# Multiplications by B half a unit ahead of their scans in place of a whole unit

## The chip, the cores and the metric

The kernel runs on one core of one Trainium2 chip. The metric is the time of one execution on the device, in microseconds (us), given as the median of several runs. The engines of the core are named as in the profile: PE (TensorE, with PEld for its weight loads), DVE (VectorE), ACT (ScalarE), POOL (GpSimd) and SP (SyncE, which here issues transfers).

## The reference

The reference is a network of four layers on four images of 64 x 64 positions with 96 channels. The last two layers are attention and a quantised feed-forward network; the change does not touch them. The first two are selective scans in four directions, and that is where the change lies. For each direction k, each of E = 192 channels and each of 16 states, the layer computes a recurrence over the 4,096 positions:

```python
def step(h, inp):
    u, d, b, c = inp
    dA = jnp.exp(d[..., None] * A)
    h = dA * h + d[..., None] * b[:, :, None, :] * u[..., None]
    y = jnp.einsum('bken,bkn->bke', h, c)
    return (h, y)
```

Here `d` is a step size computed from the image, `u` the image itself, `b` and `c` vectors of 16 states for each position. The input of the recurrence is thus the product of `d * u` (one value for each channel and position) and `b` (one value for each state and position).

## The kernel before

The kernel handles the two scan layers in four phases: two layers, each for two pairs of images. Each phase has a preparation (`prepare`: statistics, convolution, step sizes), in which `d * u` is written to memory as `du` and the step sizes as `delta`, and then a scan phase (`scan_phase`). Between them the outputs of the phase before are finished. After the fourth phase come the token layers.

A scan phase runs over 128 units: 8 chunks (`NC`) of 512 positions (`TC`), and in each chunk 16 blocks (`NEB`) of `EB` = 12 channels. The 128 partitions hold two images, four directions and 16 states. A unit passes through these steps:

- `load` fetches `dlt` (L375) and `h` (L390) through SP's queue: `h` is filled with `du`, in six transfers of 512 KB. There are four buffers of `h`. The loads of unit i+2 are recorded at the end of unit i-1 (step 11).
- `times_b` (L401, POOL) multiplies `h` by the chunk's B, in four instructions for each unit, each on `ER` = 3 of its 12 rows.
- `replicate` (L407, PE) spreads a row of `dlt` over the partitions, and `decay` (L411, ACT) makes the factor `a` of it. They run three to four rows ahead of the scan (`LEAD`).
- `scan` (L418, DVE) computes the recurrence of one row in place, from `a` in PSUM and `h` in SBUF, with the state `carry` of the chunk before. There are 12 scans in each unit.
- `contract` (L436, PE) multiplies the finished rows of the unit before by C, `evict` (L448, ACT) copies the results out, and `store` (L456) writes them with four transfers through SP's queue.
- `load_b` and `load_c` fetch B and C of a later chunk (L343); `weights` (L359, ACT) lays out C for the contractions.

The whole phase stands under `manual_schedule`: each engine executes its own instructions in the order in which the Python code records them. An instruction waits, by semaphores, for what writes its inputs and for what last uses the memory that it overwrites. The order of recording is the loop over units (`at`) and steps (`n` from 0 to 11, with `t = at * EB + n`), and `b_at(t)` is called once for each step, after the step's scan.

Of the kernel before, what the change touches and what calls it, by code (L numbers as in the profile page):

```python
# [32 lines left out]
EB = 12  # L33
NEB = E // EB
ER = EB // 4
# [5 lines left out]
NF = HID // 128  # L41
EPS = 1e-5
LEAD = 4
LN_EXP = "natural_log_exp_and_others"
SQRT_HALF = 0.7071067811865476

# [80 lines left out]
class Scans:  # L127
# [333 lines left out]
    def scan_phase(self, ph):  # L461

        nc = self.nc
        units = [self.Unit(ph, c, eb) for c in range(NC) for eb in range(NEB)]
        last = len(units)

        def ahead(t, do):
            at, n = divmod(t, EB)  # L470
            if at < last:
                do(units[at], n)

        def b_at(t):
            at, n = divmod(t, EB)
            if n % ER == 0 and 0 <= at + 1 < last:
                self.times_b(units[at + 1], n // ER)

        with self.tc.tile_pool(name="units", bufs=2) as self.units, self.tc.tile_pool(
            name="p_a", bufs=6, space=PSUM  # L480
        ) as self.p_a, self.tc.tile_pool(name="p_y", bufs=2, space=PSUM) as self.p_y:
            with self.tc.manual_schedule():
                self.start_phase(ph)
                self.load_b(ph, 0)
                self.load(units[0])
                self.load_c(ph, 0)
                self.load(units[1])
                self.load(units[2])
                self.load_c(ph, 1)
                for t in range(-EB, 0, ER):  # L490
                    b_at(t)
                for op in range(16):
                    self.weights(ph, 0, op)
                for t in range(LEAD):
                    ahead(t, self.replicate)
                for t in range(LEAD - 1):
                    ahead(t, self.decay)
                for at, u in enumerate(units):
                    before = units[at - 1] if at else None
                    for n in range(EB):  # L500
                        t = at * EB + n
                        ahead(t + LEAD, self.replicate)
                        ahead(t + LEAD - 1, self.decay)
                        self.scan(u, n)
                        q, part = divmod(n, 3)
                        if before:
                            if part < 2:
                                self.contract(before, q, part)
                            else:
                                self.evict(before, q)  # L510
                            if n == 4 and before.c < NC - 1:
                                e = before.eb * EB
                                nc.scalar.copy(
                                    ph.carry[:, e : e + EB], before.h[:, :, TC - 1]
                                )
                        b_at(t)
                        if n == 1 and u.eb >= 2 and u.c + 1 < NC:
                            self.weights(ph, u.c + 1, u.eb - 2)
                        if n == 7 and u.eb >= NEB - 2 and u.c + 1 < NC:
                            self.weights(ph, u.c + 1, u.eb)  # L520
                        if n == EB - 1:
                            if before:
                                self.store(before)
                            if u.eb == 8 and u.c + 1 < NC:
                                self.load_b(ph, u.c + 1)
                            if u.eb == NEB - 1 and u.c + 2 < NC:
                                self.load_c(ph, u.c + 2)
                            if at + 3 < last:
                                self.load(units[at + 3])
                for q in range(4):  # L530
                    self.contract(units[-1], q, 0)
                    self.contract(units[-1], q, 1)
                    self.evict(units[-1], q)
                self.store(units[-1])
# [178 lines left out]
def token_layers(ctx: ExitStack, tc, cst, a, layers, x_in, x_out):  # L713
# [51 lines left out]
    def layernorm(t, cut, out, first, **quant):  # L765
# [6 lines left out]
        with ExitStack() as order:  # L772
# [4 lines left out]
            if first:  # L777
                nc.scalar.preload_act_table_set(LN_EXP)
        var = p_a.tile([128, TC], F32, name="pa")
# [199 lines left out]
```

## Time and profile before

| what | value |
|---|---|
| median of 3 runs | 12,560.81 us |
| lowest and highest of them | 12,543.26 and 12,572.67 us |
| profiled execution, its own time | 12,532.27 us |
| profiled execution, its span | 12,530.5 us |
| PE busy | 9,786.3 us (78%) |
| DVE busy | 9,408.2 us (75%) |
| POOL busy | 7,413.5 us (59%) |
| ACT busy | 7,029.5 us (56%) |
| moved by DMA | 2,491.55 MB, mean 199 GB/s |

The span runs from the first instruction to the last of one profiled execution; its own time is 1.8 us more. The shares are means over the whole span, in which the scan phases alternate with the preparations, and the token layers follow from about 11,340 us on. What a change in the scan phases is worth must therefore be read from views cut to those phases. In a row of the groups stand the line, the engine, the operation, what it writes and reads, the number of instructions, then their busy time and the mean duration of one in ns, then the idle time of the engine just before them and what ended it.

### The profile page before, as it was taken

The numbers are of one execution on the slowest core, as the hardware profiler recorded it, in microseconds if no ns is written. First come the engines' busy times: TensorE is split into PE (matmuls) and PEld (weight loads), VectorE is DVE, ScalarE is ACT, GpSimd is POOL, SyncE is SP. The second block draws the span as 40 slices with busy tenths as digits, with TensorE's granted clock in tenths as the row PEclk, the third lists the DMA queues.
The fourth block names the chain that finished last, engine by engine and source line by source line (L and its number), as shares of the span: only waits on it lengthen the run. The fifth ranks groups of instructions, "written<-read, shape, count | busy, mean of one in ns | idle before, by whom it ended". The sixth has DMA issues, their size and how long they took to land.

```text
span 12530.5 us, 341384 instructions
## 1 busy us (share of the span) xinstructions
PE 9786.3 (78%) x147008; PEld 4985.2 (40%) x147008; DVE 9408.2 (75%) x9235; ACT 7029.5 (56%) x11815; POOL 7413.5 (59%) x2316
## 2 busy tenths in 40 slices
PE   7757788769878878869877788877877878777777
PEld 2224444433334444433334444443334444444333
DVE  2479999972569999982569999992459999994567
ACT  2356666643456666653456666662446666663456
POOL 0159888860149999870139989880118999991000
PEclk8667766679777776769777776768776676778887
DMA  3689999974679999984579999994569999994100
GB/s 93 174 223 246 239 240 242 241 183 130 201 210 248 246 248 242 243 204 125 179 206 246 244 244 245 241 227 126 159 203 236 246 245 245 246 241 134 32 21 10
DMA packets 964628, 2491.55 MB, mean 199 GB/s; under 512 B 295442, under 2 KB 578224, under 8 KB 753840
## 3 DMA queue, kind: packets, MB, share of 16 engines
q1 hardware_dynamic: 634416, 2163.45, 66.2%
q10 hardware_dynamic: 328704, 306.26, 8.4%
q8 instruction: 1158, 18.97, 0.7%
q14 instruction: 350, 2.87, 0.1%
HBM read 1955.42 MB, written 513.80 MB: 197 GB/s over the span
## 4 chain that ended last, share of the span: by engine, by line
PE 31%; DMA 28%; issue 6%; DVE 5%; SPq 4%; ACT 4%; POOL 1%; ACTq 0%; DVEq 0%; POOLq 0%
DMA h<-du 24%; PE y L436 8%; PE c L259 6%; PE a L407 5%; SPq L390 3%; PE f L586 3%; PE d L305 2%; DMA yk<-y 1%; DVE h L418 1%; PE c L288 1%; PE f L595 1%; PE f L677 1%; PE f L666 1%; PE f L652 1%; PE ph L796 1%
## 5 line engine op out<-in xcount | busy, mean ns | idle before, releaser
L401 POOL TENSOR_TENSOR h<-h,b 128x1536 f32<-128x1536 f32 x2048 | 7042.6, 3462 | 842.1 <-DMA h<-du 671.6
L418 DVE TENSOR_TENSOR_SCAN h<-a,carry,h 128x512 f32<-128x512 f32 x5376 | 6395.7, 1263 | 444.3 <-POOL h L401 329.1
L411 ACT ACTIVATE a<-a,a_col 128x512 f32<-128x512 f32 x6144 | 3939.7, 663 | 1677.4 <-PE a L407 1613.9
L436 PE MATMUL y<-h,cw 128*32 128x48 f32 x131072 | 3861.9, 268 | 1187.5 <-issue 964.3
L436 PEld LDWEIGHTS y<-h,cw 128*32 128x32 f32 x131072 | 2911.6, 138 | 3714.1 <-issue 2317.7
L407 PE MATMUL a<-dlt,rep 24*128 24x512 bf16 x6144 | 2857.7, 509 | 562.5 <-DVE h L418 466.5
L319 POOL CAST parts<-dl 96x1024 bf16<-96x1024 f32 x256 | 342.7, 1353 | 3094.3 <-DVE dl L316 2812.7
L448 ACT COPY d<-y 128x384 f32<-128x384 f32 x2048 | 980.4, 479 | 1028.8 <-PE y L436 940.8
L315 DVE TENSOR_TENSOR du_sb<-dl,xc 96x1024 f32<-96x1024 f32 x256 | 396.5, 1575 | 1292.3 <-ACT dl L313 1235.0
L259 PE MATMUL c<-xn,taps 96*96 96x512 f32 x2304 | 1034.7, 610 | 73.0 <-DVE xn L244 70.5
L418 DVE TENSOR_TENSOR_SCAN h<-a,h 128x512 f32<-128x512 f32 x768 | 863.5, 1204 | 202.7 <-ACT a L411 188.3
L407 PEld LDWEIGHTS <-rep 24*128 24x128 bf16 x6144 | 456.2, 98 | 880.6 <-issue 498.9
L305 PE MATMUL d<-xd,dt_w 7*96 7x512 f32 x1024 | 520.9, 857 | 246.5 <-ACT xd L291 220.1
L259 PEld LDWEIGHTS c<-xn,taps 96*96 96x96 f32 x2304 | 382.6, 167 | 707.8 <-issue 629.5
L818 POOL MEMSET tn<- 1x4096 f32 x8 | 28.1, 3533 | 863.6 <-PE pa L838 508.4
L586 PE MATMUL f<-yk,perm 128*128 128x384 f32 x1024 | 421.4, 552 | 92.7 <-DMA yk<-y 86.6
L266 ACT ACTIVATE xc<-c,conv_b 96x512 f32<-96x512 f32 x128 | 87.3, 682 | 721.0 <-PE c L259 661.0
L320 DVE TENSOR_TENSOR parts<-dl,parts 96x1024 bf16<-96x1024 f32 x256 | 364.8, 1446 | 155.0 <-POOL parts L319 153.4
L313 ACT ACTIVATE dl<-d 96x1024 f32<-96x1024 f32 x256 | 251.9, 1017 | 402.0 <-DMA delta<-parts 230.4
L288 PE MATMUL c<-xc,x_proj 96*103 96x512 f32 x512 | 421.6, 960 | 4.2 <-ACT xc L266 4.2
L305 PEld LDWEIGHTS d<-xd,dt_w 7*96 7x96 f32 x1024 | 151.6, 212 | 536.7 <-ACT xd L291 290.3
L359 ACT ACTIVATE cw<-c,gmask 128x256 f32<-128x256 f32 x512 | 287.1, 572 | 120.8 <-DMA h<-du 61.9
(114 smaller groups left out, 5656.4 us busy)
## 6 DMA issues: line engine op xcount, KB each, us to landing
h<-du SPq DMA_DIRECT2D x3072, 512.0 KB
delta<-parts ACTq DMA_DIRECT2D x512, 288.0 KB
dlt<-delta SPq DMA_DIRECT2D x512, 288.0 KB
du<-du_sb SPq DMA_DIRECT2D x256, 384.0 KB
du<-du_sb ACTq DMA_DIRECT2D x256, 384.0 KB
y<-d SPq DMA_DIRECT2D x2048, 48.0 KB
yk<-y SPq DMA_DIRECT2D x256, 384.0 KB
ud<-xu ACTq DMA_DIRECT2D x128, 192.0 KB
```

What stands on the lines that cost most here:

```text
L259: nc.tensor.matmul(rows(ps[:C]), taps[:, tap, h * C : (h + 1) * C], xn[:, ROWS * c + dy : ROWS * (c + 1) + dy, dx : dx + HW], start=tap == ...
L288: nc.tensor.matmul(rows(ps[:XD2]), xp[:, k, h], u[:, h], start=h == 0, stop=h == 1)
L305: nc.tensor.matmul(ps[:, m], dt_w[part, k, m * C : (m + 1) * C], xd[part], start=True, stop=True)
L315: nc.vector.tensor_tensor(rows(du), rows(delta), u, ALU.mult)
L390: nc.sync.dma_start(u.h[part, e : e + n].rearrange("p e t -> p (e t)"), ph.du[u.c][:, :, at : at + n] .rearrange("a g e t -> (a g) (e t)") ...
L401: self.nc.gpsimd.tensor_tensor(h, h, b, ALU.mult)
L407: self.nc.tensor.matmul(u.a[n], rep, u.dl[64:, n], start=True, stop=True)
L411: self.nc.scalar.activation(u.a[n], u.a[n], AF.Exp, scale=u.ph.a_col[:, at : at + 1])
L418: self.nc.vector.tensor_tensor_scan(u.h[:, n], u.a.pop(n), u.h[:, n], 0.0 if u.c == 0 else u.ph.carry[:, at : at + 1], ALU.mult, ALU.add,)
L436: self.nc.tensor.matmul(view(u.y[32 * j : 32 * j + 32], l2 * EB, (8 * EB, 4), (1, EB)), u.ph.cw[u.c][:, l1, 8 * j + l2], view(u.h, 64 * l1 ...
L448: self.nc.scalar.copy(u.d[:, :, :, l1], u.y[:, : 32 * EB].rearrange("p (t h x) -> p t h x", t=4, h=2))
L586: nc.tensor.matmul(ps[:, : 4 * C].rearrange("p (w v e) -> p w v e", w=4, v=nv), cst.perm[:, k], view(t, off, (sw if k < 2 else -sw, 4), (1 ...
```

## The change

`b_at` decides at which step of the loop the four multiplications of a unit are recorded. Before, those of unit i are recorded during unit i-1, at its steps 0, 3, 6 and 9, which is twelve scans ahead of the scan of the first row that each writes. After, they are recorded six scans ahead: the first two at steps 6 and 9 of unit i-1, the last two at steps 0 and 3 of unit i. In the prologue of a phase two multiplications of unit 0 are recorded in place of four. Number, shape and engine of the multiplications stay as they are.

```diff
@@ -41,6 +41,7 @@
 NF = HID // 128
 EPS = 1e-5
 LEAD = 4
+B_LEAD = EB // 2
 LN_EXP = "natural_log_exp_and_others"
 SQRT_HALF = 0.7071067811865476
 
@@ -472,9 +473,9 @@
                 do(units[at], n)
 
         def b_at(t):
-            at, n = divmod(t, EB)
-            if n % ER == 0 and 0 <= at + 1 < last:
-                self.times_b(units[at + 1], n // ER)
+            at, n = divmod(t + B_LEAD, EB)
+            if n % ER == 0 and 0 <= at < last:
+                self.times_b(units[at], n // ER)
 
         with self.tc.tile_pool(name="units", bufs=2) as self.units, self.tc.tile_pool(
             name="p_a", bufs=6, space=PSUM
@@ -487,7 +488,7 @@
                 self.load(units[1])
                 self.load(units[2])
                 self.load_c(ph, 1)
-                for t in range(-EB, 0, ER):
+                for t in range(-B_LEAD, 0, ER):
                     b_at(t)
                 for op in range(16):
                     self.weights(ph, 0, op)
```

## The prediction

> **What bounds the kernel now.** First the busy shares by stretch, over a long stretch of each of the four scan phases (their scans begin at 772, 3655, 6517 and 9394 us of the timeline). The view of busy time by window gives, for each, the busy time of PE, PEld, DVE, ACT and POOL, then the granted clock, the DMA share and GB/s:
>
> ```profile
> 750.00:2690.00 1940.00, 1527.07 (x33379) 822.43 (x33377) 1781.65 (x1507) 1256.72 (x2247) 1734.10 (x505) 0.69 0.95 241
> 3620.00:5530.00 1910.00, 1500.64 (x33107) 811.04 (x33107) 1764.63 (x1497) 1243.81 (x2231) 1716.88 (x500) 0.72 0.95 244
> 6490.00:8400.00 1910.00, 1497.85 (x33046) 811.92 (x33046) 1759.71 (x1490) 1245.45 (x2227) 1710.54 (x498) 0.72 0.95 242
> 9400.00:11340.00 1940.00, 1540.21 (x34294) 839.55 (x34292) 1808.34 (x1531) 1261.08 (x2262) 1740.04 (x506) 0.72 0.94 240
> ```
>
> The four stretches are 7,700 us, 61% of the span. In them the DMA engines are busy 94 to 95%, VectorE (DVE) 92 to 93%, GpSimd (POOL) 89 to 90%: three resources are near their limit, so small displacements could matter, and the question is which waits on which. The page's chain of waits and its groups answer:
>
> ```profile
> DMA h<-du 24%; PE y L436 8%; PE c L259 6%; PE a L407 5%; SPq L390 3%; PE f L586 3%; PE d L305 2%; DMA yk<-y 1%; DVE h L418 1%; PE c L288 1%; PE f L595 1%; PE f L677 1%; PE f L666 1%; PE f L652 1%; PE ph L796 1%
> L401 POOL TENSOR_TENSOR h<-h,b 128x1536 f32<-128x1536 f32 x2048 | 7042.6, 3462 | 842.1 <-DMA h<-du 671.6
> L418 DVE TENSOR_TENSOR_SCAN h<-a,carry,h 128x512 f32<-128x512 f32 x5376 | 6395.7, 1263 | 444.3 <-POOL h L401 329.1
> ```
>
> The largest single piece of the chain is the load of `h` from `du`. POOL, which multiplies `h` by B, idles 842.1 us before its multiplications, 671.6 of them for that load; VectorE, which scans `h`, idles mostly for POOL. So the order is load, then multiplication, then scan, each waiting for the one ahead.
>
> The decisive reading is how far ahead of the scans the multiplications really run. The timeline from 5100 us on, POOL's rows first and then VectorE's (start, duration, and in brackets the idle time before and what ended it):
>
> ```profile
> 5116.85 3.46 POOL L401 TENSOR_TENSOR h<-h,b 128x1536 f32<-128x1536 f32 x1 [2.71 <-DVE h L418]
> 5121.31 3.43 POOL L401 TENSOR_TENSOR h<-h,b 128x1536 f32<-128x1536 f32 x1 [1.00 <-DMA h<-du]
> 5126.49 10.26 POOL L401 TENSOR_TENSOR h<-h,b 128x1536 f32<-128x1536 f32 x3 [1.74 <-DMA h<-du]
> ...
> 5120.35 3.63 DVE L418 TENSOR_TENSOR_SCAN h<-a,carry,h 128x512 f32<-128x512 f32 x3 [2.34 <-POOL h L401]
> 5124.78 3.63 DVE L418 TENSOR_TENSOR_SCAN h<-a,carry,h 128x512 f32<-128x512 f32 x3 [0.80 <-POOL h L401]
> 5129.99 5.98 DVE L418 TENSOR_TENSOR_SCAN h<-a,carry,h 128x512 f32<-128x512 f32 x5 [1.58 <-POOL h L401]
> ```
>
> A multiplication ends at 5121.31 + 3.43 = 5124.74 and the three scans of its rows begin at 5124.78. The unit is written into the program twelve scans ahead, but it runs its own 3.46 us ahead, because its load has only just landed. The lead in time is set by the loads, not by the place in the program.
>
> **What the Trainium skill says.** "Trainium Architecture — The Big Picture", section Inside one NeuronCore: every engine has an instruction stream of its own, and streams meet only at semaphores. The trace agrees: POOL starts on a landed load (1.00 and 1.74 us of waiting above), at whatever point the other engines stand. "Perfetto Trace Analysis", section Sequencer Loop: an instruction in an engine's queue starts when its semaphores and resources are ready; the place of another engine's instruction in the source is none of these. "SBUF — State Buffer", section Who interferes with whom: a VectorE instruction with at most one SBUF input, outside the two-port modes, does not contend with GpSimd. The scan takes `a` from PSUM and `h` from SBUF (and one column of `carry`); POOL's multiplication lasts 3,414 to 3,541 ns over all 2,048, so the trace shows no blocking that a shifted overlap could alter.
>
> **The change, part by part.**
> 1. Nothing is added or removed: 4 phases x 128 units x 4 = 2,048 multiplications of 3,462 ns before and after, no DMA more or less. Cost 0.
> 2. The first two multiplications of a unit (rows 0 to 5) go from steps 0 and 3 of the unit before to steps 6 and 9 of it; the other two from its steps 6 and 9 to steps 0 and 3 of the unit itself. On POOL's own queue they pass nothing: a scan phase gives POOL no other instruction (in the groups its other work is L319, in the preparation, and L818, in the token layers). Their order among themselves stays. Cost 0, with no cover needed: the POOL stream is the same list.
> 3. On SP's queue the second pair passes what step 11 issues: four stores of `y`, one load of `dlt` and six of `h`, in some units also loads of B or C. A passed instruction could gain or lose a wait only if it touched the same buffer. The multiplications are those of unit i; the loads at the end of unit i-1 go to unit i+2, in another of the four `h` buffers. B for the next chunk is loaded after the unit with block 8, between the last use of the chunk before (blocks 14 and 15) and the first of the next one (from block 15 on), in both programs. So SP's list and its waits stay. Cost 0.
> 4. PE, ACT and VectorE: each row group is still multiplied ahead of its scan in the program (six steps, before twelve), so the scan waits for the same count of POOL's semaphore. In the prologue only two of unit 0's multiplications, in place of four, are ahead of the sixteen copies of C; those are on ACT. Cost 0.
> 5. In the two built programs the instructions of each of the five engines indeed stand in the same order, with the same waits on the same semaphore values, and on tiles at the same addresses; only the serial numbers in names differ. Thus no wait is added, and nothing queues behind one.
>
> The sum is 0 us. The profiled execution took 12,532.27 us (span 12,530.5 and 1.8 around it), which is 28.5 us (0.23%) under the median of 12,560.81. As the sum is zero, I forecast the median, rounded to 12,560.
>
> The bounds of this zero. Were a place in the program an earliest time after all, the trace bounds the loss: in the rows above the multiplications start 3.4 to 3.5 us ahead of their scans, while six scans of 1.26 us are 7.6 us, so even then the new place would be early enough there. A gain is excluded by the same list: no instruction starts on less than before.
>
> **The rivals.**
> *Slower: the place in the program holds POOL back.* It needs a wait of POOL on VectorE's step, which the old lead kept harmless. Six steps give 7.6 us; less 3.46 for the multiplication, 4.1 us remain, so it decides wherever a load is over 4.1 us late: POOL's longest wait for a load is 19.0 us, at the start. If it doubled VectorE's whole waiting for POOL (337.3 us in 456 waits, by the waits view), the time would be 12,561 + 337 = 12,898 us. For it: VectorE's largest waiting is for POOL. Against it: POOL waits for landed loads; the few times that another engine ends its wait (2.71 us for VectorE in the first row above) it is for what frees a buffer, which is the same scan or matmul before and after, and by part 5 no wait is new.
>
> *Faster: the old place made POOL wait for needless things.* The waits view shows POOL's multiplications waiting for other engines too:
>
> ```profile
> POOL h L401 <- DMA h<-du: 671.6, 737, 19.0
> POOL h L401 <- DVE h L418: 40.9, 54, 4.2
> POOL h L401 <- PE y L436: 37.8, 37, 3.4
> ```
>
> With ACT (36.7, 12.9, 3.0 and 1.5) and PE's L407 (29.0) these others come to 161.8 us. If a later place dropped them all, and all lay on the path, 12,561 - 162 = 12,399 us would result. Against it: each multiplication still waits for the load into its buffer, and that for the buffer's last readers; and a load, with DMA at 95%, comes no sooner.
>
> *The change does not do what it says* is here the forecast itself: "half a unit ahead" describes the text of the program, not a time on the chip.
>
> **How the numbers follow.** No change: 0.95; the slower and the faster rival 0.025 each, which covers a program that differs in a way I overlooked and a measurement that drifts. About 0.2% (25 us) is what a measurement of this kernel can tell from no change; the three runs before spread over 29 us. The range is the spread of a repeated kernel: from the profiled 12,532 to as much above the median, 12,590. It leaves out the two rivals, 5%, and a rare drift.
>
> **What would show it.** In the profile after: 2,048 multiplications of about 3,462 ns on POOL, idle 842 us before them give or take some tens, again mostly for the load; VectorE waiting for POOL some 330 us; multiplications that end some 0.04 us ahead of the scans they feed; the load of `h` about 24% of the chain; DMA 94 to 95% in the scan phases. Wrong would be: POOL waiting for VectorE by hundreds of us (slower rival), or its waits for PE, ACT and VectorE gone (faster rival), with the median more than 25 us off.

## The result and the profile after

The median after is 12,552.14 us over 12 runs, against 12,548.95 us over 12 runs before. The ratio is 0.9998, with a 95% interval of 0.998 to 1.0016: no change. The forecast was 12,560 us, the rounded median of the three runs known then, with a range of 12,532 to 12,590 and a chance of 0.95 for no change.

The profiled execution of the changed kernel took 12,585.92 us, in a span of 12,584.1. (One line is added near the top of the file, so each line number after it is one higher: L401 becomes L402, L418 becomes L419.) The same four stretches of the scan phases, by engine in the order PE, PEld, DVE, ACT, POOL, then the granted clock, the DMA share and GB/s:

```profile
750.00:2690.00 1940.00, 1566.06 (x33060) 820.58 (x33064) 1764.09 (x1491) 1262.42 (x2230) 1711.24 (x498) 0.63 0.95 238
3620.00:5530.00 1910.00, 1533.20 (x32527) 809.92 (x32526) 1750.49 (x1482) 1244.75 (x2209) 1685.16 (x493) 0.65 0.94 241
6490.00:8400.00 1910.00, 1521.98 (x32530) 810.92 (x32530) 1748.97 (x1482) 1239.09 (x2209) 1694.14 (x495) 0.65 0.94 243
9400.00:11340.00 1940.00, 1577.38 (x33316) 826.09 (x33316) 1776.31 (x1503) 1269.51 (x2245) 1725.11 (x502) 0.62 0.95 241
```

DMA stays at 94 to 95%, VectorE falls from 92 to 93% to about 91 to 92%, POOL from 89 to 90% to 88 to 89%. The line of busy times with the number of instructions, first from the page before and then from the page after; then from the page after its chain, the two groups, and two lines of the waits view (time waited in us, times, longest):

```profile
PE 9786.3 (78%) x147008; PEld 4985.2 (40%) x147008; DVE 9408.2 (75%) x9235; ACT 7029.5 (56%) x11815; POOL 7413.5 (59%) x2316
PE 9987.3 (79%) x147008; PEld 5008.3 (40%) x147008; DVE 9411.6 (75%) x9235; ACT 7080.6 (56%) x11815; POOL 7410.7 (59%) x2316
DMA h<-du 34%; PE y L437 9%; PE c L260 8%; PE a L408 6%; SPq L391 5%; PE f L587 2%; DVE h L419 2%; PE d L306 2%; DMA yk<-y 1%; PE c L289 1%; PE f L596 1%; PE f L678 1%; DMA delta<-parts 1%; POOL parts L320 1%; PE f L667 1%
L402 POOL TENSOR_TENSOR h<-h,b 128x1536 f32<-128x1536 f32 x2048 | 7040.5, 3461 | 889.1 <-DMA h<-du 743.7
L419 DVE TENSOR_TENSOR_SCAN h<-a,carry,h 128x512 f32<-128x512 f32 x5376 | 6397.3, 1261 | 478.8 <-POOL h L402 403.2
...
POOL h L402 <- DMA h<-du: 743.7, 779, 19.3
DVE h L419 <- POOL h L402: 429.7, 556, 3.4
```

Every engine has as many instructions as before, 341,384 in all. There are again 2,048 multiplications of 3.46 us, and POOL waits before them mostly for the load. The timeline around 1320 us, POOL's rows and then VectorE's, shows the same chain:

```profile
1317.85 3.48 POOL L402 TENSOR_TENSOR h<-h,b 128x1536 f32<-128x1536 f32 x1 [1.24 <-DMA h<-du]
1321.87 6.88 POOL L402 TENSOR_TENSOR h<-h,b 128x1536 f32<-128x1536 f32 x2 [0.53 <-DMA h<-du]
...
1321.37 3.63 DVE L419 TENSOR_TENSOR_SCAN h<-a,carry,h 128x512 f32<-128x512 f32 x3 [0.84 <-POOL h L402]
1325.37 7.16 DVE L419 TENSOR_TENSOR_SCAN h<-a,carry,h 128x512 f32<-128x512 f32 x6 [0.37 <-POOL h L402]
```

The multiplication ends at 1321.33 and its scans begin at 1321.37. Over the whole trace the lead of a multiplication (from its start to the start of the first scan of its rows) can be worked out for all 2,048:

| kernel | median lead, us | 90% are below | lead below 7.1 us | length of the four scan phases, us |
|---|---|---|---|---|
| before | 3.74 | 8.44 | 85% | 7,765 |
| after | 3.64 | 8.67 | 87% | 7,812 |

Here 7.1 us is six scans at the spacing of 1.184 us that twelve scans in 14.21 us show. Neither a whole unit (14.2 us) nor half a unit is the usual lead of either kernel. The place is not an earliest time either: in the kernel after, 305 of 2,040 multiplications (15%; the first of each phase are left out) begin before the scan six places ahead of their own has ended, the very scan behind which they are written. The slower rival needs this to be impossible.

### The profile page after: what moved, and what is told of

Read it like the earlier page. It is cut to its first block, busy times and chain, and to the rows that moved or that the text cites. A ratio compares the mean times of both kernels' runs of the same rounds, so it can differ in the third digit from the quotient of the medians.

```text
span 12584.1 us, 341384 instructions
## 1 busy us (share of the span) xinstructions
PE 9987.3 (79%) x147008; PEld 5008.3 (40%) x147008; DVE 9411.6 (75%) x9235; ACT 7080.6 (56%) x11815; POOL 7410.7 (59%) x2316
## 4 chain that ended last, share of the span: by engine, by line
DMA 40%; PE 35%; issue 7%; DVE 6%; SPq 6%; ACT 4%; POOL 1%; ACTq 1%; DVEq 0%; POOLq 0%
DMA h<-du 34%; PE y L437 9%; PE c L260 8%; PE a L408 6%; SPq L391 5%; PE f L587 2%; DVE h L419 2%; PE d L306 2%; DMA yk<-y 1%; PE c L289 1%; PE f L596 1%; PE f L678 1%; DMA delta<-parts 1%; POOL parts L320 1%; PE f L667 1%
## 5 line engine op out<-in xcount | busy, mean ns | idle before, releaser
L402 POOL TENSOR_TENSOR h<-h,b 128x1536 f32<-128x1536 f32 x2048 | 7040.5, 3461 | 889.1 <-DMA h<-du 743.7
L419 DVE TENSOR_TENSOR_SCAN h<-a,carry,h 128x512 f32<-128x512 f32 x5376 | 6397.3, 1261 | 478.8 <-POOL h L402 403.2
L408 PE MATMUL a<-dlt,rep 24*128 24x512 bf16 x6144 | 3077.6, 541 | 636.5 <-DVE h L419 536.5
L419 DVE TENSOR_TENSOR_SCAN h<-a,h 128x512 f32<-128x512 f32 x768 | 865.2, 1198 | 212.2 <-ACT a L412 146.9
```

The costliest lines, as they stand in the source:

```text
L402: self.nc.gpsimd.tensor_tensor(h, h, b, ALU.mult)
L408: self.nc.tensor.matmul(u.a[n], rep, u.dl[64:, n], start=True, stop=True)
L419: self.nc.vector.tensor_tensor_scan(u.h[:, n], u.a.pop(n), u.h[:, n], 0.0 if u.c == 0 else u.ph.carry[:, at : at + 1], ALU.mult, ALU.add,)
```

## The experiments

**A lead of three scans.**

```diff
-B_LEAD = EB // 2
+B_LEAD = 3
```

> B_LEAD = 3: each multiplication is recorded only three steps ahead of the scan that needs it, the least that the loop allows. Theory (the place in the program is not a time; every engine's list of instructions and waits is again the same as before): no change, ratio to the kernel before 1.000 within 0.003, 2,048 multiplications of about 3,460 ns, POOL idle some 840 to 900 us before them, mostly for the load of h. Rival (the place holds POOL back): a lead of three scans of 1.19 us each is 3.6 us, hardly more than one multiplication of 3.46 us, so each of 2,048 steps would lose about 1 us: some 2,000 us slower, near 14,500 us.

(Three is not the least: a multiplication is recorded after the scan of its step, so a lead of one scan would still stand ahead of the scan that needs it. Nothing below rests on this.)

Measured: 12,542.23 us median; ratio to the kernel before 0.9995, interval 0.9975 to 1.0015. Its two groups on the page:

```profile
L402 POOL TENSOR_TENSOR h<-h,b 128x1536 f32<-128x1536 f32 x2048 | 7041.1, 3462 | 899.1 <-DMA h<-du 722.4
L419 DVE TENSOR_TENSOR_SCAN h<-a,carry,h 128x512 f32<-128x512 f32 x5376 | 6396.3, 1262 | 484.8 <-POOL h L402 355.6
```

With the multiplications written three steps ahead the time is that of twelve, and the median lead on the chip is 3.75 us. Of 2,044 multiplications 1,969 begin before the scan three places ahead, behind which they are written, has ended. The rival, some 2,000 us slower, is excluded. As each engine's list is the same again, this is in effect a repeat of one program: it shows that the place of a line among the lines of other engines is not a time, but it cannot show what a real bound would cost. That is the next experiment.

**The place made into a real bound: a control, six scans and twelve scans.** On POOL, ahead of each multiplication in the loop, stands a copy of one element. In the control it reads a constant; in the others it reads the row scanned last, so that POOL, which works in order, must wait for that scan.

```diff
             if n % ER == 0 and 0 <= at < last:
+                if t >= 0:
+                    nc.gpsimd.tensor_copy(tick, units[t // EB].h[:1, t % EB, :1])
                 self.times_b(units[at], n // ER)
```

The control has `self.cst.eps[:1]` as the source; tie12 also has `B_LEAD = EB`. The tile `tick` is made once in each phase.

> B_LEAD = 6 with a copy of one element on POOL ahead of each multiplication that lies in the loop (about 2,040 of them), from a constant, so that it waits for no other engine: the price of the copy alone, the control for tie12, tie6 and tie3. Theory: the copy takes 0.1 to 0.3 us with what it leaves idle, 0.4 to 1.2 us for each unit, while POOL has about 1.5 us to spare in a unit of about 15.4 us: 0 to 1.5% slower, 12,550 to 12,740 us. Rival (POOL has no slack, every copy is on the path): 2,040 x 0.3 = 600 us slower.

> As probe6, but the copied element comes from the row that the loop scanned last, so POOL truly may not begin a multiplication until the scan six places ahead of its own is done. Theory (the loads, not the place, set when a multiplication begins, about one multiplication ahead of the scan): five scans of 1.19 us remain, 5.9 us, over the 3.46 us of a multiplication, so the wait hardly ever ends last: same as probe6 within 0.5%. Rival (a lead of half a unit is too short once it is enforced, because late loads are no longer absorbed): VectorE's waiting for POOL doubles, some 340 us (2.7%) over probe6.

> As tie6 with B_LEAD = 12: POOL may not begin a multiplication until the scan twelve places ahead of its own is done, the whole unit of the kernel before made into a real bound. Theory: the multiplications begin later than that anyway (about three scans ahead), so same as probe6 and tie6 within 0.5%. Rival: probe6 and tie12 agree and tie6 is slower by 1 to 3%.

Measured, as ratios to the kernel before: control 1.0022 (1.0009 to 1.0035), six scans 1.0018 (1.0004 to 1.0032), twelve scans 1.0014 (0.9993 to 1.0035). First the control: the busy times of its page, the group of its multiplications and VectorE's wait for POOL. Then the six-scan kernel: the groups of its multiplications and of its copies, the wait of its copies for VectorE, and VectorE's wait for POOL.

```profile
PE 9903.3 (79%) x147008; PEld 4998.0 (40%) x147008; DVE 9419.5 (75%) x9235; ACT 7064.5 (56%) x11815; POOL 7643.3 (61%) x4356
L402 POOL TENSOR_TENSOR h<-h,b 128x1536 f32<-128x1536 f32 x2048 | 7067.9, 3451 | 649.6 <-DMA h<-du 547.2
...
DVE h L419 <- POOL h L402: 367.9, 474, 3.4
```

```profile
L402 POOL TENSOR_TENSOR h<-h,b 128x1536 f32<-128x1536 f32 x2048 | 7066.8, 3451 | 538.3 <-DMA h<-du 447.2
L479 POOL COPY tick<-h 1x1 f32<-1x1 f32 x2040 | 353.5, 173 | 105.3 <-DVE h L419 104.6
...
POOL tick L479 <- DVE h L419: 104.6, 49, 14.2
DVE h L419 <- POOL h L402: 367.5, 476, 3.4
```

A copy lasts 173 ns in the profile, where it overlaps the multiplications beside it: 2,040 of them raise POOL's whole busy time by 233 us, from 7,410.7 after to 7,643.3. POOL's idle time before its multiplications shrinks by about as much, from 889.1 us after to 649.6, and the control is only 0.22% (28 us) slower. The three kernels' intervals overlap throughout.

The bound of six scans does act. None of 2,040 multiplications begins before the scan six places ahead has ended, where 249 do in the control; 90% of the leads are below 5.4 us, where 7.6 us is the control's limit; and 49 copies wait, 104.6 us in all. But VectorE loses nothing by it: it waits 367.5 us for POOL, and 367.9 in the control, where the rival had this wait doubled. What takes up the 104.6 us is not settled. The waiting for the load goes from 547.2 to 447.2 us, but with the bound of twelve scans it is as low, 458.1 us, though only four copies wait there, 28.5 us in all.

So an enforced half unit costs nothing that can be measured beside an enforced whole one. The slower rival falls twice: the studied change adds no such wait, and the wait would have cost nothing that can be measured here.

**The bound at three scans.**

```diff
-B_LEAD = EB // 2
+B_LEAD = 3
```

with the same copy of the row scanned last.

> As tie6 with B_LEAD = 3: POOL may not begin a multiplication until the scan three places ahead of its own is done. Two scans of 1.19 us remain, 2.4 us, against a multiplication of 3.46 us and some 0.2 to 0.5 us for the copy and the signals. Theory: here the place, once enforced, is shorter than the real lead, and VectorE must wait 1.2 to 1.6 us for each three rows, so a unit takes 14.2 + 5 to 6.4 = 19 to 20.6 us in place of about 15.4: 1,900 to 2,700 us slower than probe6, near 14,500 to 15,200 us, and VectorE's idle time for POOL becomes its largest. Rival (a wait on VectorE is hidden by something else): below 13,000 us.

Measured: 14,941.8 us, ratio 1.1901 (1.1883 to 1.1919). The chain of its page, VectorE's group, and its timeline (POOL's copy and multiplication, then VectorE):

```profile
POOL h L402 41%; DMA h<-du 7%; PE c L260 7%; DVE h L419 4%; PE f L590 2%; POOL tick L479 2%; SPq L391 2%; PE d L306 1%; DMA yk<-y 1%; PE c L289 1%; PE f L599 1%; PE f L681 1%; DMA delta<-parts 1%; PE f L670 1%; POOL parts L320 1%
L419 DVE TENSOR_TENSOR_SCAN h<-a,carry,h 128x512 f32<-128x512 f32 x5376 | 6509.6, 1266 | 2402.1 <-POOL h L402 2402.1
...
5103.60 0.17 POOL L479 COPY tick<-h 1x1 f32<-1x1 f32 x1 [1.38 <-DVE h L419]
5103.73 3.44 POOL L402 TENSOR_TENSOR h<-h,b 128x1536 f32<-128x1536 f32 x1
...
5102.25 3.63 DVE L419 TENSOR_TENSOR_SCAN h<-a,carry,h 128x512 f32<-128x512 f32 x3 [1.34 <-POOL h L402]
5107.21 3.63 DVE L419 TENSOR_TENSOR_SCAN h<-a,carry,h 128x512 f32<-128x512 f32 x3 [1.32 <-POOL h L402]
```

The scan that begins at 5102.25 ends about 5103.51; the copy starts at 5103.60, the multiplication ends at 5107.17, the scans begin at 5107.21, and VectorE has idled 1.32 us. Three rows take 4.96 us, so a unit takes 4 x 4.96 = 19.8 us, as expected. The load, first in the chain of the other kernels, is down to 7%, and POOL stands in its place. The number 3 is thus harmless in lead3, where it is only a place, and costs 19% here, where it is a wait. The point at which an enforced lead decides lies between three scans and six; by the sum it is where the scans that remain (2.4 us at three, 5.9 at six) fall below the 3.46 us of a multiplication with its signals, but no lead between the two was run.

**Half of the loads of `h`.**

```diff
-        u.h = self.units.tile([128, EB, TC], F32, name="h", bufs=4)
-        self.load_delta(u)
+        at = u.c * NEB + u.eb
+        if at % 2 and at > 4:
+            u.h = units[at - 4].h
+            self.load_delta(u)
+            return
+        u.h = self.units.tile([128, EB, TC], F32, name="h" + "o" * (at % 2), bufs=2)
+        self.load_delta(u)
```

> The kernel after, but every second unit from the fifth on does not load h: it multiplies and scans what is left in its buffer, so the outputs differ from the reference's; its six transfers of 512 KB are left out, all else stays. Theory (load, then multiplication, then scan, and the loads set the pace and the lead): POOL's waiting for the load of h falls from about 700 us to under 200, the multiplications run well ahead of the scans, and the scan phases go down to VectorE's own pace, 14.2 us for each unit in place of about 15.4: up to 500 us faster, I expect 12,050 to 12,350 us. Rival (POOL or PE is the bound and the loads merely look late): no change within 0.5%.

Measured: 11,958.05 us, ratio 0.9525 (0.9509 to 0.9541), 591 us faster, beyond the 12,050 to 12,350 that I expected. (`ho` is the name of `h` in every second unit.) The chain's line, VectorE's two groups, the waits for the two kinds of load, and one multiplication run and one scan run of the timeline:

```profile
DVE h L424 13%; DVE ho L424 9%; PE y L442 8%; DMA h<-du 6%; PE c L260 6%; PE a L413 5%; PE f L592 3%; POOL h L407 2%; POOL ho L407 2%; PE d L306 2%; DMA yk<-y 2%; ACT a L417 1%; SPq L396 1%; PE c L289 1%; PE f L601 1%
L424 DVE TENSOR_TENSOR_SCAN h<-a,carry,h 128x512 f32<-128x512 f32 x2688 | 3174.6, 1247 | 0.0
L424 DVE TENSOR_TENSOR_SCAN ho<-a,carry,ho 128x512 f32<-128x512 f32 x2688 | 3174.6, 1247 | 0.0
...
POOL h L407 <- DMA h<-du: 191.6, 139, 19.2
POOL ho L407 <- DMA ho<-du: 27.6, 19, 2.8
...
5105.92 3.44 POOL L407 TENSOR_TENSOR h<-h,b 128x1536 f32<-128x1536 f32 x1
...
5122.65 13.00 DVE L424 TENSOR_TENSOR_SCAN h<-a,carry,h 128x512 f32<-128x512 f32 x11
```

The load leaves the front of the chain and VectorE takes it: these scans have no idle time before them at all (0.0), where the kernel after has 478.8 us. POOL still waits 219 us for loads, a little over the 200 that I expected. The first multiplication of a unit starts at 5105.92, its scan at 5122.65: 16.7 us ahead; over all multiplications the median lead is 15.1 us, in place of 3.6. With the loads made fewer, and the multiplications recorded at the same places, the lead is four times as long, which was the central claim. The four scan phases last 7,178 us in place of 7,765 before, 587 of the 591 us: 14.0 us for each of the 512 units, from 15.2. My expectation was mis-sized: the "about 15.4" was too high, and from it to 14.2 us over 512 units would have been 614 us and not "up to 500".

**A real change of order on POOL's queue.**

```diff
-B_LEAD = EB // 2
+B_LEAD = EB
...
-                self.times_b(units[at], n // ER)
+                self.times_b(units[at], 3 - n // ER)
```

> B_LEAD = 12 as before, but the four multiplications of each unit stand in reversed order on POOL's queue (rows 9 to 11 first, rows 0 to 2 last): a change of the order on one queue, where the studied change alters none. The first scan of a unit then needs all six loads and all four multiplications. Theory: this one does move the work in time. A unit's first scan comes about 10 us later after its loads begin to land, its buffer of h comes free that much later, and the four buffers have some 13 us of slack for it, so between no change and 5% slower, I take 2% (12,800 us); VectorE's waits for POOL are longer each and fewer. Rival (the order on POOL's queue doesn't matter either): same within 0.3% and an unchanged number of waits.

Measured: 13,005.54 us, ratio 1.0358 (1.0337 to 1.0378). Two lines of its waits view, and VectorE's wait for POOL in the kernel before:

```profile
DVE h L419 <- POOL h L402: 1074.5, 355, 37.9
POOL h L402 <- DMA h<-du: 672.9, 229, 25.5
...
DVE h L418 <- POOL h L401: 337.3, 456, 3.1
```

VectorE waits for POOL 355 times, 3.0 us each in the mean, where before it waited 456 times, 0.74 us each (337.3 us). The scan phases take 8,214 us in place of 7,765, which is 449 of the 456 us. The loss is inside the expected span and over the 2% that I took. That buffers of `h` come free later, so that loads start later, was argued and not followed load by load; in keeping with it, the DMA share from 750 to 2690 us is 0.86 here and 0.95 before. The same number of equal multiplications, in another order on their own queue, does change the time: a move of this kind would have been visible, and the studied change is not one.

## Why the prediction was right

*The sum of 0.* Parts 1 to 5 held, and part 5 alone decides: the change leaves each engine the same list of instructions with the same waits, so the chip has nothing to do differently. No luck was needed, and no cost had to be hidden behind another. lead3 shows the same zero at a third size of the lead.

*The reading of the timeline.* That a multiplication runs about its own 3.46 us ahead of its scan was read from one stretch. The median over the whole trace is 3.74 us before and 3.64 us after, so it held, but as a median: 10% of the leads before are above 8.44 us. halfload shows that the loads set it. Where multiplications run further ahead than six scans, in 15% of the cases after, the place in the program does not hold them.

*The slower rival.* It was put down with 12,898 us and a limit of 4.1 us of slack. That limit was read too high. `b_at` comes after the scan of its step, so five scans are left and not six, and scans in a row are 1.184 us apart and not 1.26: 5.9 us, less 3.46 for the multiplication, leaves about 2.5. tie6 enforced this tighter bound and stayed level with its control, so the price was too high as well: VectorE's waiting for POOL did not double, it stayed at 367.5 us. The forecast did not depend on either figure. Where the bound is shorter than the multiplication (tie3), the mechanism is as described.

*The faster rival.* Waits of POOL for other engines remain after, 34.6 us for VectorE and 33.5 and 32.9 us for two lines of PE; with the same list of waits they had to.

*What the profile was to show.* POOL's idle time of 842 us "give or take some tens" was 889.1. VectorE's waiting for POOL was to be some 330 us and was 429.7, and the load's share of the chain was to be about 24% and was 34%. These two forecasts were too tight: they took one profiled execution for the rule. lead3 gives 403.0 us and 29%, again with an unchanged list of instructions. These differences are the spread between executions and no trace of the change. Of the 54 us by which the profiled execution after was longer than that before, 47 lie in the scan phases; what made them is not settled, but the 12 runs on either side show no such difference.

## What to carry to other kernels

Before costing a move in the source, ask which queue's order it changes and which wait it adds; where neither changes, as here at twelve, six and three scans, the time doesn't either. How far ahead a step really runs is read in the timeline, from the end of the producer to the start of the consumer, and is set by what the producer waits for, here the load. To test whether a lead matters, enforce it with a small dependence and run a control that pays for the instruction alone.

## What was not expected of the hardware

Two executions of the same instructions can differ a good deal in what their profiles say while their times agree: before and after differ in the granted TensorE clock (0.736 and 0.690), in PE's busy time (9,786 and 9,987 us) and in the load's share of the chain (24% and 34%), with times 0.4% apart in the two profiled executions and 0.02% apart in the ratio. What made the clock differ is not shown. And a queue that is busy for nearly 90% of a phase took in 233 us more busy time for a loss of 28 us: its waiting, mostly for the load, shrank by 240 us.
